# Giving more source-row chunks of a graph layer from GpSimd's gathers to ScalarE and VectorE

## The chip, the cores and the metric

The kernel runs on one core of a Trainium2 chip. The metric is the device time of one execution in microseconds (us); the median of three runs is compared. A core has the engines TensorE (PE; its weight loads are shown as PEld), VectorE (DVE), ScalarE (ACT), GpSimd (POOL) and SyncE (SP, used here to issue transfers). Each has an instruction queue of its own, worked off in order.

## The reference, cut to what matters

x has 12500 rows of 128 numbers; src and dst name the ends of 200000 edges, sorted by dst.

```python
h = relu(layernorm(x))                       # 12500 x 128
msgs = h[src]                                # 200000 rows, fetched by index
agg = segment_sum(msgs, dst) / max(deg, 1)   # mean over the edges of a node
t = relu(agg @ Wg + h @ Ws + bg)
t = tanh(t @ W1 + b1)                        # 128 -> 512
t = tanh(t @ W2 + b2)                        # 512 -> 512
return x + (t @ W3 + b3)
```

Everything is float32.

## The kernel before, in words

**Stages.** The layer norm goes first: x comes in pieces, h goes to a table in HBM (`htab`), and POOL meanwhile gathers the rows of 80 "raw" chunks straight from x, which are normed later. Then one long loop runs over c, the 1563 chunks of 128 edges. For every chunk, `add(c)` (L524) multiplies the chunk's 128 source rows by a one-hot matrix of their targets on PE, into a PSUM window of the current block of 512 nodes (`agg`), or into `edge` where the chunk crosses two blocks. `onehot(g)` (L433) makes the one-hot matrices of a group of GRP = 8 chunks on DVE, in three buffers, two groups ahead. `tallied` (L450) counts degrees on DVE from bytes that SP loads (`nearby`).

**Four ways to fetch the rows of a chunk.** A list LANES gives some chunks away ("apart"), the rest is gathered:

- `gather` (L350): one indirect DMA of 128 rows, issued by POOL, into one of AHEAD buffers. The gather of chunk number i of the order may start when the one AHEAD before it has been used.
- lane S, `row_loads` (L377): SP reads 32 offsets at a time into its registers and issues 128 transfers of one row.
- lane A, `column_copies(1)` (L390): a transposed copy of the table lies in SBUF (`tab`, 128 x 12544). ScalarE reads LOADS = 32 offsets into registers (`offsets`, L359) and copies 32 single columns of 4 bytes x 128 partitions (L398). Four such runs make a chunk (`cols`). `turn(c)` (L404) lets PE transpose it back, and ScalarE copies the result to SBUF (`turned`, L419).
- lane V, `column_copies(2)`: the same on DVE.

Before, every eighth chunk (c % 8 = 3, raw groups left out) from 152 to 1539 is a candidate, and of 15 candidates LANES gives seven to A, four to V, two to S. That is 77 chunks for ScalarE, 43 for VectorE, 22 for SP, and 1341 gathers.

**The order of the work** is written out by hand. `load_times` (L716) spreads the copies of a lane evenly between the uses of its chunks, MARGIN = 18 places of the order early; ScalarE gives up control after every four copies (TOGETHER), so that its activations and other copies are emitted between them; `turn` comes 9 places before the use. Both column lanes are generators: a run's offsets are loaded when the generator goes on to that run's first copies. DVE's copies are emitted right behind the one-hot of every group.

The layers of a finished block (`layers`, L698, with parts `mean`, `part0` to `part4`) are cut into single matmuls and emitted one step every second chunk (`go_on`). From chunk QUICK = 1312 on, a planner takes over: it reckons when the rows of chunk c will be there (`there`, 1.251 us a gather) and emits steps of the layers up to that time.

**tab** is filled by `own(s)`, an SP load of 512 rows of htab, and `own_turned(s)`, four PE transposes and one ScalarE copy (L419, tab), one s every four chunks: 25 of them, the last near c = 97.

Of the kernel before, what the change touches and what calls it, by code (L numbers as in the profile page):

```python
# [22 lines left out]
F32 = mybir.dt.float32  # L23
BF16 = mybir.dt.bfloat16
I32 = mybir.dt.int32
# [6 lines left out]
P = 128  # L32
# [5 lines left out]
NRAW = 10  # L38
RAW0 = 256
STEP = 40  # L40
AHEAD = 19
LATE = 12
LEAD = 16
QUICK = 1312
EVERY = 8
AT = 3
LANES = "AVASA-AVAVA-SAV"
FROM, UNTIL = 152, 1540
SBUFS = 4
MARGIN = 18  # L50
TOGETHER = 4
# [20 lines left out]
def windowed(ctx, tc, x, src, dst, Wg, Ws, bg, W1, b1, W2, b2, W3, b3, out, flag):  # L72
# [117 lines left out]
    tab = const.tile([P, NP], F32, name="tab")  # L190
    scol = const.tile([P, NCOL], I32, name="scol")
    ROWB = 4 * D
    places = [const.tile([NROW, CPR // EVERY, P], I32, name=f"place{i}") for i in range(2)]
    dloc = const.tile([P, NCOL], F32, name="dloc")
    OHS = 3
    oh_bufs = [const.tile([P, GRP, WINDOWS[0][1]], F32, name=f"oh{i}") for i in range(OHS)]
# [28 lines left out]
    with tc.tile_pool(name="setup", bufs=1) as sp, tc.tile_pool(name="ln", bufs=2) as ln:  # L225

        def indices(name, a, pad, keep):
            r = sp.tile([NROW, ROW], I32, name="idx_raw")

            nc.vector.memset(r, pad)  # L230
            even = FULL // 16 * 16
            for s0, s1 in ((0, even), (even, FULL)):
                if s1 > s0:
                    nc.scalar.dma_start(r[s0:s1, :], a[s0 * ROW : s1 * ROW].rearrange("(p e) -> p e", e=ROW))
            nc.scalar.dma_start(r[FULL : FULL + 1, :REST], a[FULL * ROW : E].rearrange("(p e) -> p e", p=1))
            if name == "src":
                some = r.rearrange("r (q p) -> r q p", p=P)[:, AT::EVERY]
                for to, step, first_at in zip(places, (ROWB, 4), (0, TAB_AT)):
                    nc.vector.tensor_scalar(to, some, float(step), float(first_at), op0=ALU.mult, op1=ALU.add)
            else:  # L240
                r8 = flat(oh_bufs[0]).bitcast(U8)[:NROW, :ROW]
                nc.scalar.copy(r8, r.bitcast(U8).rearrange("r (e b) -> r e b", b=4)[:, :, 0])
                end = back + NROW * ROW
                nc.scalar.dma_start(bytes_at[back:end].rearrange("(r e) -> r e", e=ROW), r8)
                past = flat(oh_bufs[1]).bitcast(U8)[:1, : max(back, reads)]
                nc.vector.memset(past, PAST)
                nc.scalar.dma_start(bytes_at[:back].rearrange("(o e) -> o e", o=1), past[:, :back])
                nc.scalar.dma_start(bytes_at[end:].rearrange("(o e) -> o e", o=1), past[:, :reads])
            rf = sp.tile([NROW, ROW], F32, name="idx_f")
            nc.vector.tensor_copy(rf, r)  # L250
            for q0 in range(0, CPR, 4):
                p = ps_m.tile([P, 4, P], F32, name="pm")
                for q in range(4):
                    nc.tensor.transpose(p[:, q, :NROW], rf[:, (q0 + q) * P : (q0 + q + 1) * P], ident[:NROW, :NROW])  # L254
                keep(q0, p[:, :, :NROW].rearrange("p q r -> p r q"))


        def by_row(t):
            return t.rearrange("p (r q) -> p r q", q=CPR)

        def keep_src(q0, p):
            nc.vector.tensor_copy(by_row(scol)[:, :, q0 : q0 + 4], p)

        def keep_dst(q0, p):
            nc.vector.tensor_tensor(
                by_row(dloc)[:, :, q0 : q0 + 4], p, by_row(low)[:, :, q0 : q0 + 4], op=ALU.subtract
            )


        pieces = [(0, 4), (4, PIECE - 4)] + [(t, min(PIECE, NT - t)) for t in range(PIECE, NT, PIECE)]  # L270
        for i, (t0, k) in enumerate(pieces):
            xt = ln.tile([P, PIECE, D], F32, name="xt", bufs=3)
            whole = min(N - t0 * P, k * P) // P
            rest = min(N - t0 * P, k * P) - whole * P
            if rest:
                nc.vector.memset(xt[:, whole, :], 0.0)
            nc.sync.dma_start(xt[:, :whole, :], x[t0 * P : (t0 + whole) * P, :].rearrange("(t p) d -> p t d", p=P))
            if rest:
                nc.sync.dma_start(xt[:rest, whole, :], x[(t0 + whole) * P : N, :])
            if i == 1:  # L280
                indices("src", src, 0, keep_src)
            stats = ps_a.tile([P, BLK], F32, name="agg")[:, : 2 * k].rearrange("p (s t) -> p s t", s=2)
            xt = xt[:, :k]
            centre(ln, xt, k, stats)
            factors(stats)
            h = ln.tile([P, PIECE, D], F32, name="h", bufs=2)
            scale(h[:, :k], xt, k, stats)
            nc.sync.dma_start(htab[t0 * P : (t0 + k) * P, :].rearrange("(t p) d -> p t d", p=P), h[:, :k])


        low = sp.tile([P, NCOL], F32, name="low")
        nc.vector.tensor_copy(row_f, row_i)
        nc.vector.tensor_tensor(
            by_row(low), row_f[:, :, None].to_broadcast([P, NROW, CPR]), q_i[:, None, :].to_broadcast([P, NROW, CPR]),
            op=ALU.add,
        )
        for c0, w in WINDOWS[1:]:
            v = low[:, c0:]
            nc.vector.tensor_scalar(v, v, float(first(w) - window(c0 - 1)[0] + per * (c0 - 1)), None, op0=ALU.add)
        indices("dst", dst, pad_dst, keep_dst)  # L300
        steps, at = (t[:, RAW0:RAW1].rearrange("p (u k) -> p u k", k=STEP) for t in (dloc, low))
        nc.vector.tensor_copy(near, steps[:, :, :GRP])
        nc.vector.scalar_tensor_tensor(
            steps[:, :, :GRP], rdst, float(first(WINDOWS[0][1]) - first(W_RAW, per * GRP)),
            at[:, :, :1].to_broadcast([P, NRAW, GRP]), op0=ALU.add, op1=ALU.subtract,
        )
# [52 lines left out]
    def offsets(lane, c, p0):  # L359
        step, first_at = (4, TAB_AT) if lane else (ROWB, 0)  # L360
        r, q = divmod(c, CPR)
        kind = (mybir.EngineType.SP, mybir.EngineType.Activation, mybir.EngineType.DVE)[lane]
        loads, vs = nc.values_load_multi_w_load_instructions(  # L363
            places[min(lane, 1)][r : r + 1, q // EVERY, p0 : p0 + LOADS], engines=[kind], min_val=first_at,
            max_val=first_at + (N - 1) * step,
            skip_runtime_bounds_check_because="src holds rows of x, as the indirect DMAs take it to",
        )
        for ld in loads:
            if lane == 2 and last:
                tc.add_manual_dep(  # L370
                    ld.ins, last[0].ins.name,
                    mybir.DependencyInfo(mybir.DependencyClass.NoSync, mybir.DependencyReason.DATA), reason="issue_after",
                )
            tc.keep_in_program_order(ld)
        return enumerate(vs, p0)

    def row_loads(lane):  # L377
        for c in lanes[lane]:
# [3 lines left out]
            for p0 in range(0, P, LOADS):  # L382
                for p, v in offsets(lane, c, p0):
                    sp_dma(rb[p : p + 1, :], hbytes[bass.ds(v, ROWB)].rearrange("(o b) -> o b", o=1))
                    if (p + 1) % TOGETHER == 0:
                        yield

    columns, last = {}, []

    def column_copies(lane):  # L390
        copy = nc.scalar.copy if lane == 1 else nc.vector.tensor_copy
        for c in lanes[lane]:
            t = ed.tile([P, P], F32, name=f"cols{lane}", bufs=2)
            columns[c] = t
            tb = t.bitcast(U8)
            for p0 in range(0, P, LOADS):
                for p, v in offsets(lane, c, p0):
                    done = tc.keep_in_program_order(copy(tb[:, 4 * p : 4 * p + 4], tbytes[:, bass.ds(v - TAB_AT, 4)]))  # L398
                    if lane == 2:
                        last[:] = [done]  # L400
                    if (p + 1) % (TOGETHER if lane == 1 else LOADS) == 0:
                        yield

    def turn(c):  # L404
        pt = ps_m.tile([P, 4, P], F32, name="pm")
# [6 lines left out]
    class act:  # L412


        def activation(*a, **k):
            tc.keep_in_program_order(nc.scalar.activation(*a, **k))  # L416

        def copy(*a):
            tc.keep_in_program_order(nc.scalar.copy(*a))  # L419
# [319 lines left out]
    def soonest():  # L739
        two = work[: 2 if len(work) > 1 and work[1][3] < work[0][3] and work[0][4] else 1]  # L740
        return min(two, key=lambda w: max(w[2], now), default=None)
# [20 lines left out]
    for c in range(NCH):  # L762
# [34 lines left out]
        if c >= QUICK:  # L797

            there = 7.5 + 1.251 * (NRAW * GRP + order.index(c)) if c not in apart else 0
            while soonest() and max(now, soonest()[2]) < there:  # L800
                go_on(soonest())
            now = max(now, there) + 0.27
# [11 lines left out]
        if c % TILE_EVERY == 1 and c // TILE_EVERY < NT:  # L814
            tallied(c // TILE_EVERY)
            if c // TILE_EVERY + 2 < NT:
                seen(c // TILE_EVERY + 2)
        if c % 4 == 2 and c // 4 + 1 < nown:
            own_turned(c // 4 + 1)
            if c // 4 + 3 < nown:  # L820
                own(c // 4 + 3)
        if c < QUICK:
            if c % 2 == 0:
                go_on(work[0] if work else None)
# [380 lines left out]
```

## Time and profile before

| | before |
|---|---|
| runs, us | 1816.99, 1815.15, 1812.56; median 1815.15 |
| profiled execution, us | 1817.22 (span 1815.4, mean PE clock granted 0.889) |
| PE busy | 1299.8 us, 72% |
| DVE busy | 1152.6 us, 63% |
| ACT busy | 1187.4 us, 65% |
| POOL busy | 1348.7 us, 74% |
| DMA | 163.06 MB, mean 90 GB/s |

The span runs from the first to the last instruction of the profiled execution. A line of a group reads: line of the kernel, engine, operation, output <- inputs, count | busy us, mean ns of one | idle time of the engine just before them, and what released it. "issue" is time in which the engine waited for nothing that the profile shows: register loads, branches and the issue of instructions are not counted as busy. A line of the waits reads: engine, tile and line <- what it waited for: total us, times, longest. A line of the timeline begins with start and duration in us; equal instructions that follow one another are merged (x32), and the idle time before them stands in brackets.

### The profile page before, as it was taken

The numbers are of one execution on the slowest core, as the hardware profiler recorded it, in microseconds if no ns is written. First come the engines' busy times: TensorE is split into PE (matmuls) and PEld (weight loads), VectorE is DVE, ScalarE is ACT, GpSimd is POOL, SyncE is SP. The second block draws the span as 40 slices with busy tenths as digits, with TensorE's granted clock in tenths as the row PEclk, the third lists the DMA queues.
The fourth block names the chain that finished last, engine by engine and source line by source line (L and its number), as shares of the span: only waits on it lengthen the run. The fifth ranks groups of instructions, "written<-read, shape, count | busy, mean of one in ns | idle before, by whom it ended". The sixth has DMA issues, their size and how long they took to land.

```text
span 1815.4 us, 36659 instructions
## 1 busy us (share of the span) xinstructions
PE 1299.8 (72%) x5031; PEld 812.2 (45%) x5031; DVE 1152.6 (63%) x6351; ACT 1187.4 (65%) x10333; POOL 1348.7 (74%) x1429
## 2 busy tenths in 40 slices
PE   0046767777888787877777777777777767698598
PEld 0035544444555554444444444444444344454457
DVE  7946845668677788766756666756666764644411
ACT  1201145867878788878777777778768865777763
POOL 7777777777777777777777777777777776777773
PEclk9996565989898899989999889989889998798899
DMA  8844423233333332332332332332333323222221
GB/s 211 235 140 112 122 68 80 75 81 81 81 94 94 86 102 75 94 88 74 84 84 75 87 88 75 86 82 76 86 81 81 92 71 86 67 72 66 65 59 37
DMA packets 135577, 163.06 MB, mean 90 GB/s; under 512 B 32934, under 2 KB 99107, under 8 KB 135128
## 3 DMA queue, kind: packets, MB, share of 16 engines
q0 software_dynamic: 45472, 93.22, 20.4%
q1 hardware_dynamic: 86574, 63.90, 12.4%
q10 hardware_dynamic: 3276, 3.51, 0.7%
q14 instruction: 213, 1.74, 0.3%
q8 instruction: 42, 0.69, 0.2%
HBM read 147.49 MB, written 13.03 MB: 88 GB/s over the span
## 4 chain that ended last, share of the span: by engine, by line
DMA 26%; PE 24%; issue 20%; ACT 16%; POOL 8%; DVE 3%; ACTq 1%; DVEq 0%; POOLq 0%
DMA rows<-htab,scol 26%; ACT cols L398 14%; PE pm L342 14%; PE agg L342 7%; POOL rows L352 4%; POOL raw L167 4%; PE edge L342 2%; ACT h L416 2%; DVE cols L398 1%; DVE nearby L452 1%; DVE oh L438 1%; ACTq L363 1%; PE pt L345 1%; PE pm L345 0%; DVEq L363 0%
## 5 line engine op out<-in xcount | busy, mean ns | idle before, releaser
L352 POOL DMA_INDIRECT rows<-htab,scol x1341 | 1270.7, 948 | 416.7 <-issue 230.2
L398 ACT COPY cols<-tab 128x4 uint8 x9856 | 996.4, 190 | 283.3 <-issue 231.7
L342 PE MATMUL pm<-h,w 128*128 128x512 f32 (+4 forms) x1344 | 648.3, 580 | 36.1 <-ACT h L416 22.2
L342 PE MATMUL agg<-oh,rows 128*128 128x144 f32 (+3 forms) x1914 | 474.9, 352 | 231.7 <-DMA rows<-htab,scol 224.3
L342 PEld LDWEIGHTS agg<-oh,rows 128*128 128x128 f32 x1914 | 353.6, 224 | 509.1 <-DMA rows<-htab,scol 370.2
L398 DVE COPY cols<-tab 128x4 uint8 x5504 | 432.2, 196 | 164.1 <-issue 142.9
L438 DVE TENSOR_TENSOR oh<-shared,dloc 128x1152 f32<-128x1152 f32 (+2 forms) x186 | 245.7, 1322 | 358.0 <-PE agg L342 217.1
L452 DVE TENSOR_SCALAR_CACHE_REDUCE nearby<-nearby,parity 128x2416 uint8<-128x2416 uint8 x98 | 266.2, 2717 | 4.8 <-DMA nearby<-bytes_at 4.8
L342 PEld LDWEIGHTS pm<-h,w 128*128 128x128 f32 x1344 | 222.1, 204 | 60.2 <-ACT h L416 26.5
L342 PE MATMUL edge<-oh,rows 128*128 128x144 f32 (+2 forms) x768 | 178.6, 332 | 80.9 <-DMA rows<-htab,scol 80.1
L342 PEld LDWEIGHTS edge<-oh,rows 128*128 128x128 f32 x768 | 131.7, 209 | 192.7 <-DMA rows<-htab,scol 126.7
L416 ACT ACTIVATE h<-pm,b2c 128x512 f32<-128x512 f32 (+4 forms) x112 | 70.2, 626 | 63.9 <-PE pm L342 63.8
L419 ACT COPY tab<-pt 128x512 f32<-128x512 f32 (+1 forms) x25 | 14.4, 577 | 127.2 <-PE pt L345 127.2
L167 POOL DMA_INDIRECT raw<-in_x_dram,rsrc x80 | 77.1, 964 | 25.6 <-issue 23.5
L416 ACT ACTIVATE h<-pm,b1c 128x512 f32<-128x512 f32 (+4 forms) x112 | 68.9, 627 | 29.1 <-PE pm L342 28.7
L254 PE MATMUL pm<-ident,idx_f 98*128 98x98 f32 x32 | 6.2, 376 | 77.8 <-DVE agg L220 47.5
L345 PE MATMUL pm<-ident,cols 128*128 128x128 f32 x120 | 35.6, 297 | 32.1 <-DVE rd L511 15.7
L342 PEld LDWEIGHTS agg<-oh,turned 128*128 128x128 f32 x176 | 36.6, 227 | 36.5 <-issue 24.7
L342 PE MATMUL agg<-oh,turned 128*128 128x144 f32 (+1 forms) x176 | 42.4, 328 | 11.3 <-ACT turned L419 11.3
L573 DVE TENSOR_TENSOR mT<-agg,sums 128x136 f32<-128x136 f32 (+6 forms) x57 | 15.2, 271 | 40.6 <-PE agg L342 31.3
L254 PEld LDWEIGHTS pm<-ident,idx_f 98*128 98x128 f32 x32 | 5.1, 223 | 78.6 <-issue 47.8
L688 DVE TENSOR_TENSOR o<-pt,xb 128x512 f32<-128x512 f32 x23 | 15.7, 681 | 35.3 <-PE pt L345 34.9
(90 smaller groups left out, 632.6 us busy)
## 6 DMA issues: line engine op xcount, KB each, us to landing
srows<-htab SPq DMA_DIRECT2D x2816, 0.5 KB
nearby<-bytes_at SPq DMA_DIRECT2D x98, 302.0 KB
rows<-htab,scol POOLq DMA_INDIRECT x1341
xb<-htab SPq DMA_DIRECT2D x24, 256.0 KB
xb<-in_x_dram SPq DMA_DIRECT2D x23, 256.0 KB
out_dram<-o SPq DMA_DIRECT2D x23, 256.0 KB
xt<-in_x_dram SPq DMA_DIRECT2D x7, 704.0 KB
htab<-h SPq DMA_DIRECT2D x7, 704.0 KB
```

Source lines behind the costliest of these rows:

```text
L167: nc.gpsimd.indirect_dma_start(out=t[:, j, :], out_offset=None, in_=x, in_offset=bass.IndirectOffsetOnAxis(ap=rsrc[:, g, j : j + 1], axis=0),)
L342: tc.keep_in_program_order(nc.tensor.matmul(*a, **k))
L345: tc.keep_in_program_order(nc.tensor.transpose(*a, **k))
L352: nc.gpsimd.indirect_dma_start(out=r, out_offset=None, in_=htab, in_offset=bass.IndirectOffsetOnAxis(ap=scol[:, c : c + 1], axis=0),)
L363: loads, vs = nc.values_load_multi_w_load_instructions(places[min(lane, 1)][r : r + 1, q // EVERY, p0 : p0 + LOADS], engines=[kind], min_v ...
L398: done = tc.keep_in_program_order(copy(tb[:, 4 * p : 4 * p + 4], tbytes[:, bass.ds(v - TAB_AT, 4)]))
L416: tc.keep_in_program_order(nc.scalar.activation(*a, **k))
L419: tc.keep_in_program_order(nc.scalar.copy(*a))
L438: newest[:] = [nc.vector.tensor_tensor(oh[:, :k, :w], lane[:, None, :w].to_broadcast([P, k, w]), dloc[:, g * GRP : g * GRP + k][:, :, None ...
L452: done = nc.vector.tensor_scalar(w, w, parity[:, t % 2 : t % 2 + 1], None, op0=ALU.is_equal, op1=ALU.add, accum_out=degs[:, t : t + 1])
L573: nc.vector.tensor_tensor(out, s, t, op=ALU.add)
L688: nc.vector.tensor_tensor(o[:, :whole], po[:, :whole], xb[:, :whole], op=ALU.add)
```

## The change

- Candidates are every fourth chunk (EVERY = 4), so two of a group may be given away, from chunk 104. The new list of 30 gives eight to A, six to V, two to S: 91 chunks for ScalarE, 67 for VectorE, 23 for SP; 1302 are gathered. SP's are only taken where c % 8 = 3, since its table of places keeps the old step.
- `own` and `own_turned` run every second chunk, the last near c = 47.
- AHEAD is 17 instead of 19.
- ScalarE's offsets of the next run are loaded behind an activation of the layers, if the run before is used up by then; otherwise as before, with the first copies.
- At chunk 1312 the planner's clock is set SPREAD = 8 us back.

```diff
-AHEAD = 19
+AHEAD = 17
...
-EVERY = 8
+SPREAD = 8
+EVERY = 4
 AT = 3
-LANES = "AVASA-AVAVA-SAV"
-FROM, UNTIL = 152, 1540
+LANES = "A-V-A-S-AV-A-V-A-V-AS-VA--A-V-"
+FROM, UNTIL = 104, 1540
...
-    places = [const.tile([NROW, CPR // EVERY, P], I32, name=f"place{i}") for i in range(2)]
+    steps_of = (GRP, EVERY)
+    places = [const.tile([NROW, CPR // k, P], I32, name=f"place{i}") for i, k in enumerate(steps_of)]
+    assert all(c % GRP == AT for c in lanes[0])
...
-            places[min(lane, 1)][r : r + 1, q // EVERY, p0 : p0 + LOADS], engines=[kind], min_val=first_at,
+            places[min(lane, 1)][r : r + 1, q // steps_of[min(lane, 1)], p0 : p0 + LOADS], engines=[kind], min_val=first_at,
...
+    def runs(lane):
+        for c in lanes[lane]:
+            for p0 in range(0, P, LOADS):
+                yield c, p0, list(offsets(lane, c, p0))
+
+    scalar_runs, loaded = runs(1), []
+
+    def load_offsets():
+
+        if not loaded:
+            loaded.extend(r for r in [next(scalar_runs, None)] if r)
...
+        vector_runs = runs(2)
+        while True:
+            if lane == 1:
+                load_offsets()
+                run = loaded[0] if loaded else None
+            else:
+                run = next(vector_runs, None)
+            if run is None:
+                return
+            c, p0, offs = run
+            if p0 == 0:
+                columns[c] = ed.tile([P, P], F32, name=f"cols{lane}", bufs=2)
+            tb = columns[c].bitcast(U8)
+            for p, v in offs:
+                done = tc.keep_in_program_order(copy(tb[:, 4 * p : 4 * p + 4], tbytes[:, bass.ds(v - TAB_AT, 4)]))
+                if lane == 2:
+                    last[:] = [done]
+                if lane == 1 and p + 1 == p0 + LOADS:
+                    loaded.clear()
+                if (p + 1) % (TOGETHER if lane == 1 else LOADS) == 0:
+                    yield
...
         def activation(*a, **k):
             tc.keep_in_program_order(nc.scalar.activation(*a, **k))
+            load_offsets()
...
+            if c == QUICK:
+                now = there - SPREAD
...
-        if c % 4 == 2 and c // 4 + 1 < nown:
-            own_turned(c // 4 + 1)
-            if c // 4 + 3 < nown:
-                own(c // 4 + 3)
+        if c % 2 == 1 and c // 2 + 1 < nown:
+            own_turned(c // 2 + 1)
+            if c // 2 + 3 < nown:
+                own(c // 2 + 3)
```

More of the change, by code (lines that the diff above doesn't have):

```diff
@@ L236, in indices @@
             if name == "src":
-                some = r.rearrange("r (q p) -> r q p", p=P)[:, AT::EVERY]
-                for to, step, first_at in zip(places, (ROWB, 4), (0, TAB_AT)):
-                    nc.vector.tensor_scalar(to, some, float(step), float(first_at), op0=ALU.mult, op1=ALU.add)
+                chunks = r.rearrange("r (q p) -> r q p", p=P)
+                for to, k, step, first_at in zip(places, steps_of, (ROWB, 4), (0, TAB_AT)):
+                    nc.vector.tensor_scalar(to, chunks[:, AT::k], float(step), float(first_at), op0=ALU.mult, op1=ALU.add)
             else:
@@ L388, in windowed @@
     columns, last = {}, []
+    def runs(lane):
[6 more added lines that the diff above has]
+            loaded.extend(r for r in [next(scalar_runs, None)] if r)
     def column_copies(lane):
         copy = nc.scalar.copy if lane == 1 else nc.vector.tensor_copy
[L392 to L402, printed above, removed]
+        vector_runs = runs(2)
[19 more added lines that the diff above has]
+                    yield
     def turn(c):
```

## The prediction

> **What bounds the kernel now.** I read the page first, then the same engines over a stretch in the middle (300 to 1500 us), then the waits in that stretch, then single instructions. From the page, the span and three groups (idle time of the engine stands behind the bar):
>
> ```profile
> span 1815.4 us, 36659 instructions
> ...
> L352 POOL DMA_INDIRECT rows<-htab,scol x1341 | 1270.7, 948 | 416.7 <-issue 230.2
> L398 ACT COPY cols<-tab 128x4 uint8 x9856 | 996.4, 190 | 283.3 <-issue 231.7
> ...
> L398 DVE COPY cols<-tab 128x4 uint8 x5504 | 432.2, 196 | 164.1 <-issue 142.9
> ```
>
> Three engines fetch source rows: POOL by 1341 gathers, ScalarE (ACT) by 77 chunks of 128 copies, VectorE (DVE) by 43 chunks. POOL's own timeline, first gathers, its only long stall, and its last:
>
> ```profile
> 104.58 0.94 POOL L352 DMA_INDIRECT rows<-htab,scol  x1 [0.30 <-issue]
> ...
> 1532.15 0.94 POOL L352 DMA_INDIRECT rows<-htab,scol  x1 [6.80 <-PE agg L342]
> ...
> 1790.68 0.94 POOL L352 DMA_INDIRECT rows<-htab,scol  x1 [0.30 <-issue]
> ```
>
> In the stretch 300 to 1500 the windows view counts 961 gathers:
>
> ```profile
> core 0: us, PE busy (x) PEld busy (x) DVE busy (x) ACT busy (x) POOL busy (x), PEclk, DMA share, GB/s
> 300.00:1500.00 1200.00, 914.31 (x3483) 544.45 (x3482) 828.96 (x5136) 913.05 (x8289) 906.97 (x961) 0.92 0.32 84
> ```
>
> 1200 / 961 = 1.249 us each. The waits of the same stretch (total, times, longest):
>
> ```profile
> POOL rows L352 <- issue: 165.6, 543, 0.3
> ...
> PE agg L342 <- DMA rows<-htab,scol: 171.2, 245, 2.7
> ```
>
> POOL never waits over 0.3 us here, and TensorE (PE) waits for the rows that POOL fetches. So **POOL sets the pace now**. But look at the same answer for ScalarE:
>
> ```profile
> ACT cols L398 <- issue: 185.2, 200, 1.8
> ACT h L416 <- PE pm L342: 57.1, 32, 4.5
> ACT cols L398 <- ACT cols L398: 38.9, 46, 1.0
> ACT turned L419 <- PE pm L345: 3.0, 3, 1.4
> ACT cols L398 <- ACT h L416: 2.0, 4, 0.7
> ```
>
> 76% busy looks like room. It is not: 185.2 + 38.9 + 2.0 = 226 us are the gaps ahead of copies, in which the engine loads offsets into registers. 913 + 226 = 1139 us of 1200 are spent; what waits for another engine is 57.1 + 3.0 = 60 us. ScalarE is 95% full, just under POOL.
>
> **The change, part by part.**
>
> *POOL.* 39 gathers fewer (1341 to 1302) at 1.249 us: -48.7 us, if POOL keeps the pace. The stall of 6.80 us may go too (below). POOL alone would thus bring 1815.15 to about 1760.
>
> *ScalarE's columns.* 77 to 91 chunks: 14 x 4 = 56 more runs of 32 copies with a load of offsets each. The start of the column work, and its last copies:
>
> ```profile
> 201.23 0.39 ACT L419 COPY sums<-edge 128x280 f32<-128x280 f32 x1 [0.76 <-PE edge L342]
> ...
> 245.40 0.69 ACT L416 ACTIVATE h<-pm,b1c 128x512 f32<-128x512 f32 x1 [2.89 <-PE pm L342]
> 247.65 3.14 ACT L398 COPY cols<-tab 128x4 uint8 x32 [1.56 <-issue]
> 251.72 3.14 ACT L398 COPY cols<-tab 128x4 uint8 x32 [0.94 <-issue]
> 255.81 3.14 ACT L398 COPY cols<-tab 128x4 uint8 x32 [0.94 <-issue]
> ...
> 1757.66 0.46 ACT L398 COPY cols<-tab 128x4 uint8 x4
> ```
>
> Run to run is 4.08 us (3.14 of copies, 0.94 of load): 16.3 us a chunk, 56 x 4.08 = +228.5 us. Inside a run the starts lie (3.14 - 0.19) / 31 = 95 ns apart, though one copy lasts 190 ns by the group's row: they overlap. [...]
>
> *"Loads behind activations."* Can the load's 0.94 us be hidden? The row pair to look at is a load soon after an activation:
>
> ```profile
> 713.42 0.68 ACT L416 ACTIVATE h<-pm,b1c 128x512 f32<-128x512 f32 x1
> 714.00 0.85 ACT L398 COPY cols<-tab 128x4 uint8 x8
> 715.29 2.76 ACT L398 COPY cols<-tab 128x4 uint8 x28 [0.44 <-issue]
> ```
>
> Here the gap is 0.44 us: while the activation executes, the queue gets about 0.5 us ahead. So the idea works where it happens. But the new code loads at an activation only if the run before is used up, which it is in one of eight places; and where that is so, the old code's load, emitted with the next copies, followed the same activation. Counted in the built order of ScalarE's instructions: loads of offsets directly behind an activation of the layers are 20 of 308 before and 18 of 364 after; with at most eight copies between, 62 and 67. The edit hides nothing new. I cost it at 0; the ends are 0 and 0.5 us on each of the 192 loads that have an activation since the load before (-96 us).
>
> *The smaller items on ScalarE.* 38 more copies of turned chunks up to the last column copy (119 to 157) at up to 0.257 us by their group's row, 0.16 where the neighbours overlap it: +6 us.
>
> ```profile
> L419 ACT COPY turned<-pm 128x128 f32<-128x128 f32 x120 | 30.8, 257 | 5.4 <-PE pm L345 5.2
> ```
>
> In the new order the first offsets are loaded right behind the copy to sums at 201.23, ahead of the five activations and the table load that end at 246.1; those now lie within the column work: at 0.69 us and less for each, and with the table load, some +4.5 us (between 3 and 6).
>
> *The sum on ScalarE.* The column stage lasts from 246.1 to 1758.1 = 1512 us. In it ScalarE waited for PE:
>
> ```profile
> ACT h L416 <- PE pm L342: 77.9, 47, 5.1
> ...
> ACT sums L419 <- PE edge L342: 17.3, 1, 17.3
> ACT turned L419 <- PE pm L345: 3.8, 4, 1.4
> ```
>
> 99 us in all, so work is 1413 us. After: 1413 + 228.5 + 6 + 4.5 = 1652 us, from 201.6 (44.5 us earlier): the last column copy ends at 1854 if ScalarE waits for nothing. An engine that runs late finds its matmuls done, so most of the 99 us go; I keep 30 and say 1884. Behind that copy comes the tail:
>
> ```profile
> 1758.00:1815.40 57.40, 48.83 (x365) 45.21 (x364) 8.16 (x35) 19.27 (x56) 25.47 (x27) 0.98 0.18 46
> ```
>
> PE works 48.8 of these 57.4 us. The last chunk given to ScalarE is 1539 both times, with 23 gathers behind it and nearly the same PE instructions, so the tail stays between 48.8 and 57.4: I take 55. Span 1939. The profiled execution took 1.8 us more than its span (1817.2), and 2.1 us more than the median of the runs shown, so the forecast for the median is **1939 us**.
>
> A check by the pattern of lanes: 120 chunks outside the raw groups held 107 gathers (133.7 us) and 7 ScalarE chunks; now 104 gathers (129.9 us) and 8. ScalarE's work was 1139 / 1200 x 133.7 = 126.9 us, and is now 126.9 + 16.3 + 0.5 = 143.7: 13.8 us over POOL, in 1356 / 120 = 11.3 patterns 156 us over the 1760 of POOL's pace: 1916, without waits.
>
> *VectorE's columns.* 43 to 67 chunks. Waits and column time in 300 to 1500:
>
> ```profile
> DVE oh L438 <- PE agg L342: 123.6, 45, 6.9
> DVE cols L398 <- issue: 116.1, 114, 2.7
> DVE oh L438 <- PE edge L342: 80.2, 31, 7.0
> ...
> sum 1200.00, PE 28.56 PEld 14.51 DVE 362.43 ACT 808.55; mean PE 28.56 PEld 14.51 DVE 362.43 ACT 808.55
> ```
>
> Columns take 362 + 116 = 478 us with their load gaps; all work is 829 + 116 = 945 of 1200, or 105.3 us a pattern, of which 53.3 are four chunks. Six chunks: 105.3 + 26.7 = 132 us, at least, since some smaller gaps come on top. That is above POOL's 129.9, too, and 8% under ScalarE's 143.7: hidden, but barely. What is queued behind the added runs is the next group's onehot, for which PE waits; two groups of lead cover it.
>
> *The rest.* The own tiles are turned every second chunk instead of every fourth, so tab is ready near chunk 47 instead of 97, which the start at 104 needs. PE has the room: it waits for rows. SP, however, fetches these tiles behind the nearby loads, and waited there:
>
> ```profile
> SPq L348 <- DVE nearby L452: 16.4, 4, 9.6
> ```
>
> Tiles are now fetched about 5 us ahead instead of 10, so PE may wait a few us, four times; 14 gathers' lead (17 us) covers it. I take 0 and keep +10 for the high end. AHEAD 17 for 19 takes 2.5 us of lead from POOL; only the 6.80 us stall shows POOL short of buffers: 0. SPREAD lets part of the layers' burst at chunk 1312 start 8 us earlier in the planner's time: that burst made the waits before 1532 (17.3 and 6.80), and what it saves is inside the 99 us already. One chunk more on SP's rows and the larger place table are off every path: 0.
>
> **The rivals.**
>
> 1. *POOL stays the bound, and the kernel gets faster.* It needs ScalarE's load gaps to vanish behind other work: 364 x 0.94 = 342 us are there to be had. Break-even with 1815 lies at 1939 - 1815 = 124 us, 0.34 us less on every load. Below that the time goes to 1760, or to 1760 + 11.3 x (132 - 129.9) = 1784 if VectorE then binds. Against it: the built order, and 0.94 us in rows where nothing else stood in the queue. [...] Chance 0.06.
> 2. *Loads behind activations hide in part.* A ScalarE that no longer waits at activations keeps its 0.5 us of lead on more of the 192 loads; 62 had it before, so up to 130 x 0.47 = 61 us less: about 1878. Chance 0.12.
> 3. *VectorE and ScalarE pass their delays on.* Both over 90% full, tied through PE: onehots come late, PE waits, ScalarE's 99 us stay: 1854 + 99 + 57 = 2010 at the top, 1975 halfway. For it: VectorE's margin of 8% or less. Against it: two groups of lead. Chance 0.2.
> 4. *The forecast*, 1900 to 1965. Chance 0.62.
>
> **How the numbers follow.** The likeliest is 1939. The range takes in rival 2 at the low end and most of rival 3 at the high one: 1875 to 1995. Rival 1 alone can end below the time before: faster by over 0.3% (about what a measurement of this kernel can tell from no change) 0.05, within it 0.01, slower 0.94.
>
> **What would show it.** Right: ScalarE's load gaps stay near 0.94 us, 364 of them; its waits for PE shrink below 60 us; the last column copy ends near 1884; POOL shows long stalls on PE (over 100 us in all), PE waits for ScalarE's cols, turned or h instead of for rows. Rival 1: load gaps below 0.6 us, POOL at 1.249 us without stalls. Rival 2: many gaps of 0.4 us. Rival 3: PE waiting on oh, ScalarE still waiting near 100 us. A price of a run other than 4.08 us, or a busier start before 201 us, would move the number without changing the cause.

## The result, and the profile after

The changed kernel takes 1967.83 us (median of 4 runs, 1965.57 to 1969.77), the kernel before 1816.07 us: a ratio of 1.0839, 95% interval 1.0819 to 1.0859. The forecast was 1939 us with a range of 1875 to 1995. The profiled execution took 1965.57 us, its span is 1963.7 us.

The page's groups of the three engines that fetch rows (idle time behind the bar), and how its chain of waits is shared out:

```profile
ACT 52%; issue 16%; DVE 16%; PE 8%; DMA 4%; SPq 3%; ACTq 2%; DVEq 1%; POOL 0%; POOLq 0%
...
L355 POOL DMA_INDIRECT rows<-htab,scol x1302 | 1234.3, 948 | 596.1 <-PE agg L345 228.7
L422 ACT COPY cols<-tab 128x4 uint8 x11648 | 1174.2, 190 | 315.0 <-issue 250.2
L422 DVE COPY cols<-tab 128x4 uint8 x8576 | 665.8, 195 | 231.0 <-issue 217.3
```

POOL now idles 596 us where it was 417. Some 0.3 us ahead of each gather are in both; what is new are 89 stalls of over 0.35 us in its timeline, 229 us in all (before: 2, 8 us), nearly all of them until PE frees a buffer. In the stretch 300 to 1500 us, the windows and the waits of POOL and PE:

```profile
300.00:1500.00 1200.00, 806.13 (x3194) 527.46 (x3193) 910.08 (x6779) 942.66 (x8707) 802.41 (x850) 0.83 0.29 75
```

```profile
POOL rows L355 <- PE agg L345: 157.9, 196, 8.9
...
POOL rows L355 <- PE edge L345: 55.3, 63, 9.8
...
PE pm L348 <- ACT h L442: 103.8, 31, 9.4
PE pm L345 <- ACT h L442: 63.3, 25, 8.0
PE pm L345 <- ACT turned L446: 58.6, 21, 12.8
PE pm L348 <- ACT turned L446: 55.6, 23, 5.1
PE pm L345 <- DVE rd L538: 40.5, 7, 9.4
```

850 gathers in 1200 us is 1.41 us each, not 1.249. Before, PE waited here for gathered rows (171.2 us); that wait has no line any more. PE waits for ScalarE's h and turned, and POOL for PE. ScalarE in its column stage (212 to 1902 us):

```profile
ACT cols L422 <- issue: 250.2, 285, 1.9
ACT cols L422 <- ACT cols L422: 54.3, 64, 1.0
ACT h L442 <- PE pm L345: 34.2, 17, 6.1
ACT shared L222 <- DVE oh L465: 23.9, 1, 23.9
ACT sums L446 <- PE edge L345: 15.4, 2, 15.2
ACT cols L422 <- ACT turned L446: 7.1, 8, 0.9
ACT turned L446 <- PE pm L348: 3.8, 2, 2.6
```

The load gaps are still there: 250.2 + 54.3 + 7.1 and 2.9 in smaller lines = 314.5 us over 364 loads, 0.86 us each (0.89 in some of the expectations below); before, 0.92. ScalarE's wait for PE's matmuls in this stage fell from 77.9 to 34.2 us. In 300 to 1500 us it spends 943 us on work and 227 on load gaps, 1169 of 1200: its queue is the bound, as forecast. Where the 29 us above the forecast lie, its timeline shows:

```profile
212.41 0.39 ACT L446 COPY sums<-edge 128x280 f32<-128x280 f32 x1 [15.22 <-PE edge L345]
214.66 3.14 ACT L422 COPY cols<-tab 128x4 uint8 x32 [1.86 <-issue]
...
1900.68 0.85 ACT L422 COPY cols<-tab 128x4 uint8 x8
```

- The column work starts at 212.8 instead of 201.6: +11 us.
- It lasts to 1901.5, 1689 us instead of 1652 + 30: +7 us. Waits were 62 us (34.2 + 23.9 + 3.8; the 15.2 lie ahead of the start), work 1627.
- The tail behind it is 62.2 us instead of 55: +7 us. The rest, 4 us, lies outside the span and between this execution and the median.

### The profile page after: what moved, and what is told of

Its sections match the earlier page's. It is cut to its first block, busy times and chain, and to the rows that moved or that the text cites. A ratio compares the mean times of both kernels' runs of the same rounds, so it can differ in the third digit from the quotient of the medians.

```text
span 1963.7 us, 41992 instructions
## 1 busy us (share of the span) xinstructions
PE 1250.2 (64%) x5069; PEld 836.7 (43%) x5069; DVE 1377.5 (70%) x9423; ACT 1364.5 (69%) x12163; POOL 1312.5 (67%) x1390
## 4 chain that ended last, share of the span: by engine, by line
ACT 52%; issue 16%; DVE 16%; PE 8%; DMA 4%; SPq 3%; ACTq 2%; DVEq 1%; POOL 0%; POOLq 0%
ACT cols L422 45%; DVE cols L422 7%; ACT h L442 5%; PE pm L345 5%; DVE nearby L479 3%; DVE oh L465 2%; DMA xt<-in_x_dram 2%; SPq L351 2%; ACTq L366 2%; DMA xb<-htab 1%; PE agg L345 1%; ACT turned L446 1%; DVEq L366 1%; PE pt L348 1%; PE edge L345 1%
## 5 line engine op out<-in xcount | busy, mean ns | idle before, releaser
L355 POOL DMA_INDIRECT rows<-htab,scol x1302 | 1234.3, 948 | 596.1 <-PE agg L345 228.7
L422 ACT COPY cols<-tab 128x4 uint8 x11648 | 1174.2, 190 | 315.0 <-issue 250.2
L422 DVE COPY cols<-tab 128x4 uint8 x8576 | 665.8, 195 | 231.0 <-issue 217.3
L345 PE MATMUL pm<-h,w 128*128 128x512 f32 (+4 forms) x1344 | 700.6, 619 | 197.4 <-ACT h L442 120.3
L345 PE MATMUL agg<-oh,rows 128*128 128x144 f32 (+3 forms) x1878 | 386.7, 327 | 23.3 <-DMA rows<-htab,scol 22.5
L348 PE MATMUL pm<-ident,cols 128*128 128x128 f32 x158 | 51.7, 327 | 168.5 <-ACT h L442 79.3
L345 PE MATMUL edge<-oh,rows 128*128 128x144 f32 (+2 forms) x726 | 143.8, 313 | 5.9 <-DMA rows<-htab,scol 5.6
L348 PEld LDWEIGHTS pm<-ident,cols 128*128 128x128 f32 x158 | 24.2, 153 | 187.1 <-ACT h L442 88.5
L348 PE MATMUL pm<-ident,degs 128*128 128x128 f32 x99 | 22.2, 359 | 66.1 <-ACT h L442 49.3
L348 PE MATMUL pt<-ident,xb 128*128 128x128 f32 x98 | 24.1, 393 | 59.6 <-DMA xb<-htab 45.1
```

The source lines that it names most:

```text
L345: tc.keep_in_program_order(nc.tensor.matmul(*a, **k))
L348: tc.keep_in_program_order(nc.tensor.transpose(*a, **k))
L355: nc.gpsimd.indirect_dma_start(out=r, out_offset=None, in_=htab, in_offset=bass.IndirectOffsetOnAxis(ap=scol[:, c : c + 1], axis=0),)
```

## The experiments

Each is an edit of the changed kernel; all times are medians beside the kernel before on the same chip, where that took 1817 to 1819 us, except where said.

**e1: without loads behind activations.**

```diff
         def activation(*a, **k):
             tc.keep_in_program_order(nc.scalar.activation(*a, **k))
-            load_offsets()
```

> The changed kernel without the call that loads ScalarE's offsets behind an activation. Theory (ScalarE's queue is the bound, and moving the loads hides nothing new): the loads directly behind an activation were 18 of 364, so 1968 us within 6. Rival (the moved loads hide 0.5 us each on many of the 192 loads with an activation before them): up to 96 us slower, 2000 us or more; if the moved loads hold up activations instead: 1955 us or less.

1967.43 us, against 1967.83 with it. This part of the change does nothing here, as its 18 places in the built order said.

**e2: one load a chunk instead of four.**

```diff
-                yield c, p0, list(offsets(lane, c, p0))
+                if lane != 1 or p0 == 0:
+                    kept = [v for _, v in offsets(lane, c, p0)]
+                yield c, p0, list(enumerate(kept, p0))
```

> ScalarE loads offsets only for the first 32 columns of a chunk and uses them again for the other 96 (so three quarters of its columns are copies of wrong rows; the copies themselves stay). 273 of 364 loads go, at a measured gap of 324/364 = 0.89 us: 243 us less for ScalarE, 122 us a pattern, below POOL's 129.9 and VectorE's 132. Theory: the time falls until POOL or VectorE binds, 1760 to 1830 us. Rival (VectorE's added runs are the bound): 1930 us or more. Rival (the load gaps are hidden elsewhere): no change.

1789.36 us, ratio 0.9840 (0.9822 to 0.9859). This kernel leaves 273 loads out, so that three quarters of ScalarE's columns hold wrong rows, and keeps every copy; 178 us go. The changed kernel's loss hangs on ScalarE's queue, and its load gaps are enough to make it. AHEAD = 17 and SPREAD, which were not tried alone, are in this kernel, too, so they don't make the loss. What comes next (windows, then waits, 300 to 1500):

```profile
300.00:1500.00 1200.00, 889.69 (x3555) 548.09 (x3556) 1007.62 (x7601) 1041.27 (x9777) 892.75 (x946) 0.91 0.32 84
...
DVE cols L424 <- issue: 162.5, 143, 2.8
DVE oh L467 <- PE edge L345: 11.2, 6, 4.0
DVE oh L467 <- PE agg L345: 6.4, 3, 3.2
...
PE agg L345 <- DMA rows<-htab,scol: 108.1, 155, 3.1
...
PE pm L345 <- DVE mT L604: 70.1, 10, 10.6
```

VectorE is 1008 us busy and has 163 us of load gaps: 1170 of 1200, and hardly a wait for PE to free a one-hot buffer (17.6 us, before 213 with three lines). But POOL is back at 1200 / 946 = 1.268 us a gather, near its 1.249, and PE waits for its rows again. So both are nearly full, and which of the two binds isn't shown.

**e3: seven A in the pattern.**

```diff
-LANES = "A-V-A-S-AV-A-V-A-V-AS-VA--A-V-"
+LANES = "A-V-A-S-AV-A-V---V-AS-VA--A-V-"
```

> One A of the pattern's eight goes to a gather: 80 chunks for ScalarE, 67 for VectorE, 23 for SP, 1313 gathers. Theory: ScalarE drops to 143.7 - 16.3 = 127.4 us a pattern, under POOL (105 gathers, 131.1) and VectorE (132 or more): 1785 to 1825 us. Rival (VectorE is the bound of the changed kernel, too): 1940 us or more.

1849.84 us, ratio 1.0171 (1.0152 to 1.0190): 118 us less for 11 chunks fewer, so the direction is ScalarE's, but 25 us above my upper end, and still above the kernel before. See e9.

**e4: four V in the pattern.**

```diff
-LANES = "A-V-A-S-AV-A-V-A-V-AS-VA--A-V-"
+LANES = "A-V-A-S-AV-A---A-V-AS-VA--A---"
```

> Two V of the pattern's six go to gathers: 45 chunks for VectorE or so, 91 for ScalarE, about 1324 gathers. Theory: ScalarE's 143.7 us a pattern stay the bound, above POOL's 132.4: 1940 to 1970 us. Rival (VectorE's added runs pass their delays on to PE and ScalarE): below 1900 us.

1941.12 us. VectorE's added runs are not the bound, but they do cost: 27 us. The waits of ScalarE and VectorE (300 to 1500) say how:

```profile
300.00:1500.00 1200.00, 826.43 (x3278) 541.09 (x3277) 778.21 (x4852) 965.87 (x8937) 841.62 (x893) 0.84 0.30 78
...
ACT cols L422 <- issue: 186.7, 215, 1.6
ACT cols L422 <- ACT cols L422: 34.7, 41, 1.0
...
ACT h L442 <- PE pm L345: 3.2, 5, 1.2
...
DVE oh L465 <- PE agg L345: 177.2, 43, 17.7
```

VectorE has time again, and ScalarE's activations wait 3.2 us for PE instead of 26; over the whole column stage, with turned, 11.4 instead of 38.0, which is the 27 us. 966 busy + 187 + 35 + 9 of smaller gaps = 1197 of 1200 us: a full queue.

**e5 to e8: a disturbed chip.** Four kernels ran on a chip where the kernel before itself took 2494 us. e5 and e6 changed when own tiles are turned, and e6 the lanes:

```diff
-        if c % 2 == 1 and c // 2 + 1 < nown:
-            own_turned(c // 2 + 1)
-            if c // 2 + 3 < nown:
-                own(c // 2 + 3)
+        if c % 3 == 2 and c // 3 + 1 < nown:
+            own_turned(c // 3 + 1)
+            if c // 3 + 3 < nown:
+                own(c // 3 + 3)
...
-LANES = "A-V-A-S-AV-A-V-A-V-AS-VA--A-V-"
+LANES = "A-V-A-S-AV-A-V---V-AS-VA--A---"
```

e7 loads ScalarE's offsets 16 at a time; e8, besides, up to three loads ahead of their copies:

```diff
+SOME = 16
...
-            for p0 in range(0, P, LOADS):
+            for p0 in range(0, P, SOME if lane == 1 else LOADS):
...
-        if not loaded:
+        if len(loaded) < 3:
```

> The changed kernel with an own tile turned every third chunk instead of every second, so each is fetched 7.5 us ahead instead of 5. Theory: PE's 45 us of waits for these tiles shrink, ScalarE's column work starts near 203 instead of 214.7 us, and since ScalarE is the bound from there on, the end moves with it: 1955 to 1963 us. Rival (the early stall is made up later): 1968 us, no change.

> Own tiles every third chunk, and a pattern of seven A, five V and two S in 30: ScalarE 127.4 us a pattern, VectorE some 120, POOL 106 gathers = 132.4. Theory: POOL is the bound again with some 28 gathers fewer than before: 1780 to 1800 us, faster than both kernels. Rival (VectorE's runs still pass delays on, as with seven A and six V): 1820 us or more.

> ScalarE's offsets in 728 loads of 16 instead of 364 of 32; the copies stay the same. What does a load's gap of 0.89 us depend on? If on the load itself: 364 x 0.89 = 324 us more, near 2290 us. If on the number of registers: 1968 us. Halfway: 2130 us.

> As the kernel with loads of 16, but up to three loads may stand ahead of their copies, so that nearly every activation has a load directly behind it (226 of 728 instead of 75). Theory (a load directly behind an activation hides about 0.5 us, and the changed kernel merely has too few such places): some 150 x 0.45 = 70 us less than with loads of 16. Rival (nothing is hidden): the same time as with loads of 16.

Measured: 2639.95, 2563.49, 2563.28 and 2582.92 us. In e5's timeline of ScalarE copies of one and the same run stand apart, where nothing lies between them in the queue:

```profile
907.78 0.19 ACT L422 COPY cols<-tab 128x4 uint8 x1 [0.22 <-issue]
908.49 0.19 ACT L422 COPY cols<-tab 128x4 uint8 x1 [0.52 <-issue]
909.21 0.29 ACT L422 COPY cols<-tab 128x4 uint8 x2 [0.52 <-issue]
```

What held them up isn't shown; the times of these four runs decide nothing. e6 and e8 were run again; e5 and e7 weren't. e9 below has e5's own tiles, with other lanes, on another chip: its first column copies start at 223.68 us, 9 us later than the changed kernel's 214.66, where e5's expectation had 203. What the tiles do alone to the time stays open.

**e9: e6 again.** Edit as above.

> The mix of seven A, five V and two S with own tiles every third chunk once more, since on the chip of the run before the kernel before itself took 2494 us. Theory: with ScalarE at 127 us a pattern, VectorE at some 120 and POOL at 132.4, POOL is the bound again: 1780 to 1800 us, faster than both kernels. Rival (VectorE's runs still pass delays on, as with seven A and six V): 1820 us or more.

1847.82 us, ratio 1.0171 (1.0157 to 1.0185). The expectation failed. It failed like e3, with one V less and VectorE's queue no fuller than 894.5 + 140.5 = 1035 of 1200 us, so a full VectorE is hardly why. I had balanced a whole pattern. Both kernels drop the A in the middle and leave the others where they were, three or four places apart with one gap of eight, and a chunk's copies must be done between one use and the next. From its POOL timeline, the mean time from one gather to the next by place in the pattern (one place is four chunks, chunks 160 to 1300):

```
e9, places 0 to 9: 1.25   10: 1.34   11: 1.45   12: 1.37   13 to 16: 1.25
    17: 1.34   20: 1.41   22: 1.36   24: 1.37   27: 1.38   28: 1.31   29: 1.35
    the others: 1.25 to 1.28
```

POOL runs at full pace in some stretches and stalls behind the crowded A at 8 and 11 and at 19, 23 and 26: three places are 12 chunks, some 13 us of gathers, against 16.3 us for a ScalarE chunk. That the spacing is the cause is argued from this table; an evenly spaced seven wasn't tried.

**e10: e8 again.** Edit as above.

> Loads of 16, up to three ahead of their copies, 226 of 728 directly behind an activation, once more for the same reason. If a load's gap is one of the load itself (0.89 us), some 150 us slower than the changed kernel: 2120 us or more. If it goes by the registers (0.45 us for 16), and a load directly behind an activation is hidden whole, ScalarE saves up to 226 x 0.45 = 100 us against the changed kernel, less what that hid already: 1880 to 1940 us. If it goes by the registers and nothing is hidden: 1968 us.

1835.89 us, ratio 1.0112 (1.0097 to 1.0128): 132 us less than the changed kernel with the same lanes, and 44 us below the lowest time that I had expected. Its load gaps of 300 to 1500 us:

```profile
ACT cols L424 <- issue: 16.9, 44, 0.9
```

17 us in place of some 226. But only 226 of the 728 loads stand behind an activation; the others vanished, too. Size or place?

**e11: small loads, in the old places.** ScalarE 16 at a time, VectorE 8.

```diff
+SOME = (32, 16, 8)
...
-            for p0 in range(0, P, LOADS):
+            for p0 in range(0, P, SOME[lane]):
```

> The changed kernel, lanes and all, with ScalarE's offsets in loads of 16 and VectorE's in loads of 8 instead of 32. If the gaps of small loads are gone, as they nearly were with loads of 16 ahead, ScalarE needs some 143.7 - 32 x 0.89 = 115 to 121 us a pattern and VectorE some 107, both under POOL's 129.9: POOL is the bound, 1760 to 1790 us, faster than both kernels. Rival (what helped was the loading ahead, not the size): 1960 us or more.

1827.09 us, ratio 1.0041 (1.0025 to 1.0058). It is the size: with loads where the changed kernel has them, ScalarE's gaps are gone (7 us below). But the time stops just above the kernel before, and the 1760 to 1790 us that I expected are missed. The windows, then the waits of VectorE, ScalarE and PE (300 to 1500):

```profile
300.00:1500.00 1200.00, 825.94 (x3463) 546.93 (x3464) 1032.62 (x7334) 1026.52 (x9428) 866.32 (x918) 0.84 0.31 81
...
DVE cols L423 <- issue: 108.3, 421, 0.7
DVE oh L466 <- PE agg L346: 44.8, 18, 2.9
...
ACT cols L423 <- issue: 6.8, 16, 0.9
...
PE pm L346 <- DVE rd L539: 109.1, 11, 16.7
PE pm L349 <- DVE rd L539: 93.1, 7, 19.0
```

On VectorE a gap at a load of 8 was still 0.26 us by mean (108.3 / 421). Against e10, where it loads 32 at a time, its gaps fall from 160 to 108 us, but its busy time rises from 976 to 1033 us for the same number of column copies, so its share isn't relieved: 1033 + 108 = 1141 of 1200 us, against 1136. PE now waits for rd, the degrees of a block, which VectorE copies behind its column runs. That VectorE passes its delay on is rival 3's idea, though by rd and not by one-hots. It is not shown to be what holds e10 and e11 up: in e2 VectorE was fuller (1170 us), PE waited for its mT (70 us) but not for rd, and the time was 38 us shorter than e11's. Why rd comes late here and not there stays open.

**e12: the gap by size.** ScalarE's offsets of a chunk in six loads, in a single run.

```diff
+SIZES = (8, 32, 16, 32, 24, 16)
...
+            p0 = 0
+            for some in SIZES if lane == 1 else [LOADS] * (P // LOADS):
+                yield c, p0, list(offsets(lane, c, p0, some))
+                p0 += some
```

> ScalarE's 128 offsets of a chunk in loads of 8, 32, 16, 32, 24 and 16, one behind the other, to read the gap by size. [...] Rival (a load waits where its registers and those of the run before don't fit in together): no gap for 32 behind 8 or behind 16, a gap for 24 behind 32.

```profile
814.71 4.35 ACT L425 COPY cols<-tab 128x4 uint8 x44
819.97 2.00 ACT L425 COPY cols<-tab 128x4 uint8 x20 [0.91 <-issue]
821.88 0.67 ACT L445 ACTIVATE h<-pm,b2c 128x512 f32<-128x512 f32 x1
822.46 1.22 ACT L425 COPY cols<-tab 128x4 uint8 x12
824.16 0.48 ACT L425 COPY cols<-tab 128x4 uint8 x4 [0.47 <-issue]
824.54 0.26 ACT L449 COPY turned<-pm 128x128 f32<-128x128 f32 x1
824.70 4.36 ACT L425 COPY cols<-tab 128x4 uint8 x44
830.00 0.69 ACT L425 COPY cols<-tab 128x4 uint8 x4 [0.95 <-issue]
```

1889.29 us, 79 less than the changed kernel, where my estimate, from a price of a load by size that no run shows, was some 100. Read the rows by counts: 20 + 12 = 32 copies behind a gap of 0.91, 24 behind 0.47, and 4 + 44 = 48 copies, which are 24 + 16 + 8, without a gap at the loads of 16 and 8. Then the next 32, 0.95. Over the whole run 81 of the 91 loads of 24 show a gap, by median 0.47 us, and 179 of the 182 of 32, by median 0.97 behind 8 and 0.92 behind 16; of the 182 loads of 16 only 4 do, of the 91 of 8 one. So from 24 to 32 registers the gap grew by (0.93 - 0.47) / 8 = 0.058 us a register, for 8 and 16 there was nearly always none, and for 32 it was much the same behind 8 as behind 16: the rival, which had no gap for 32 behind 8, falls.

The loads of 16 weren't free. In two places where the activation ahead of a load had itself waited for PE, no row of copies ran meanwhile, and more of the load showed: 1.41 us in the changed kernel with 32 registers, then 0.43 us in e11 with 16:

```profile
1092.59 0.69 ACT L442 ACTIVATE h<-pm,b1c 128x512 f32<-128x512 f32 x1 [2.74 <-PE pm L345]
1094.69 2.76 ACT L422 COPY cols<-tab 128x4 uint8 x28 [1.41 <-issue]
...
1037.40 0.69 ACT L443 ACTIVATE h<-pm,b1c 128x512 f32<-128x512 f32 x1 [13.85 <-PE pm L346]
1038.52 3.07 ACT L423 COPY cols<-tab 128x4 uint8 x28 [0.43 <-issue]
```

From start to start that is 2.10 us for 32 and 1.12 us for 16 registers, 0.061 us a register. Behind copies, the next copy starts 0.19 + 0.94 = 1.13 us after the last one, so by estimate 2.10 - 1.13 = 0.97 us more of a load of 32 are covered there: about ten copies at 95 ns. That these are copies already in ScalarE's queue is argued, not shown.

## Why the prediction was right, and where its steps were off

- *POOL sets the pace before, ScalarE is 95% full*: held. Relieved of loads (e2) the kernel drops below the time before. Relieved of 11 chunks (e3) it loses 118 of the 152 us, but stays above it.
- *Run price 4.08 us, sum 1652 us of work*: measured 1627. The loads' gaps were 0.86 us, not 0.92 and more: 51 of 363 gaps are under 0.6 us, before 30 of 308. That is rival 2's mechanism, worth some 20 us here instead of 61; the likely reason, that more loads came soon after an activation that didn't wait, is argued.
- *Loads behind activations hide nothing new*: shown by e1.
- *Most of the 99 us of waits go; I keep 30*: 62 were left. 24 of them are one wait of ScalarE's activation of the raw rows' statistics for VectorE's one-hot (24 in e4, too), and 27 of the rest go with two V (e4). So VectorE's added chunks cost 27 us on top; they are not the cause. Waits 32 us too low and work 25 us too high nearly cancel: that the stage came out only 7 us long is luck.
- *Own tiles: "I take 0"* was 11 us too low, the largest part of the 29. The waits of PE and SP from 95 to 260 us:

```profile
PE pt L348 <- DMA xb<-htab: 45.1, 16, 24.8
...
SPq L351 <- DVE nearby L479: 14.3, 2, 14.1
```

  SP stood 14.1 us behind VectorE's nearby, PE 24.8 us for one tile. The lead of 14 gathers did not cover it: POOL, which had no stall of over 0.35 us in this window before, stood 7.68, 2.81, 1.63 and 0.72 us for PE, and ScalarE's start stood behind PE as well (the 15.22 us above).
- *Tail 55 us*: 62.2, above the 57.4 that were to be its upper end. PE is busy 54 of them where it was 48.8, at a granted clock of 0.88 where it was 0.98.

```profile
1901.50:1963.70 62.20, 53.95 (x366) 50.14 (x364) 8.00 (x35) 18.72 (x55) 24.53 (x26) 0.88 0.15 40
```

- *Rival 1*: it lost, as expected, but "0.94 us in rows where nothing else stood in the queue" was read wrongly. A gap of 0.94 us looked like a load that nothing covers; by the rows behind e12 it is what remains of a longer one (2.10 us from start to start behind an activation that had waited) after some 0.97 us, about ten copies at 95 ns, are covered; that is my estimate from those rows. So my step from a gap of 0.94 us to a load that nothing covers was wrong; what it lacked was the length of a load. The prediction's sum stood because it used the measured gap and not my picture of it.
- *The pattern check* (1916 without waits) served for the changed kernel, whose A are three or four places apart throughout. Used for e3 and e9 it missed by 25 and 48 us.

No version tried with all the work kept beats the kernel before; e11 comes to within 0.4%. Of the gain that 39 fewer gathers promise (49 us), the changed kernel sees nothing, because POOL no longer sets the time.

## What to carry to other kernels

Count an engine's gaps for register loads as work before giving it more: ScalarE showed 76% busy and was 95% full, and the added lane was paid in full. A gap read behind a row of copies can be only the part of a load that they don't cover (for 32 registers here 0.94 us behind copies, 1.41 us behind an activation that had waited), so test its size dependence before pricing the same load in another place. And balance a handed-over share over every stretch between two uses, not over a whole pattern; e3 and e9 point to that, though an even seven wasn't tried.

## What the hardware showed that I had not expected

- ScalarE's register loads behind copies 95 ns apart: a gap at 1 of 91 loads of 8 registers and at 4 of 182 of 16, 0.47 us for 24, some 0.93 us for 32 (e12). Behind an activation that had waited, 32 registers took 2.10 us from start to start (changed kernel) and 16 took 1.12 (e11). Halving the load to 16 took the gaps from 227 to 7 us in 1200 (e11).
- VectorE, which does 32 column copies in some 2.4 to 2.7 us where ScalarE takes 3.14 (changed kernel), shows by mean 0.26 us for a load of 8 (e11) and by mean 1.06 us for one of 32 (155.4 / 147 in the changed kernel); splitting there moved the time from gaps to busy time and gained nothing.
- One chip ran the kernel before in 2494 us instead of 1817; e5's trace from there has gaps of 0.5 us between copies of one run.
